# The last batch element in two halves of its tokens, and sums of 8 by TensorE in three groups of sixteen

## The chip, the cores and the metric

One core of a Trainium2 chip runs the whole kernel. The metric is the device time of one execution in microseconds. The kernel before took 3622.65 us, the median of three runs (3621.72 to 3628.54).

## What is computed

The input x has 8 batch elements of 512 tokens with 256 features. Each element goes through four steps, each with a layer norm in front and added back to x:

```
x = x + attention_a(layernorm(x))   # per token: 16 heads; q, k, v have 64 numbers each
x = x + ffn(layernorm(x))
x = x + attention_b(layernorm(x))   # over the tokens: 16 heads of 16, causal
x = x + ffn(layernorm(x))

# attention_a, for each token and head, with 64 queries and 64 keys that are single numbers:
scores[q, k] = Q[q] * K[k] / 8, masked to k <= q
attn[q] = sum_k softmax(scores)[q, k] * V[k]

# ffn (1024 hidden, ternary weights):
h = silu(w1 x * s1) * (w2 x * s2);  h = gelu(h1 h * s);  h = gelu(h2 h * s);  w3 h * s3
```

Attention A mixes nothing between tokens: it takes the features of one token alone. Attention B needs all earlier tokens of its element. The first FFN needs its own tokens alone.

## The kernel before

**Two programs in one order.** Attention A runs in groups: a group is one element b, one tile i of 128 tokens and one set g of four heads, so an element has 16 groups (`self.todo` in `AttentionA.__init__`, L722). Everything that follows attention A (first FFN, attention B, second FFN, written as Python generators `ffn` and `attention_b`) belongs to the element before, and is called the B stream here. The order of instructions on PE, DVE, ACT and POOL is written out by hand.

**Slots.** A table (`G['order']`, with one of its own for the first element) gives each step of a group a slot. Group n starts at slot 12 n; `slot(t)` calls the steps that are due, of several groups at once, in the table's order. A group's steps run from about slot -8 (`project`, the q, k and v products) to slot 36 (`new_x`, which writes the group's part into x). After each slot the main loop at the end of `fast_path` advances the B stream: each `yield` gives a number of units, `step_of` scales them by `pace`, and the loop goes on until the units spent reach `total` (304.8 for an element's 192 slots) times the slots gone, 33 slots and one element late.

**Attention A in a group.** The triangle of 64 x 64 scores is cut into squares of 32, 16, 8, 4, 2 and 1 (`units`). `scores` multiplies queries with keys (on POOL for the large squares, on DVE for the unit of 8 and below, whose tile is `ws`), `exps` is ACT's exponential, `weigh` multiplies with values on DVE. Then the sums over keys. For squares of 32 and 16 a DMA that adds (`halve`) first folds a tile in two; then `fold` on POOL, `gather` (L1047, a reduction on DVE), or `sums32` (L918): 16 transposing products against the identity that add up in PSUM, a copy by ACT (`keep_sums`), a transpose back (`turn_sums`) and one addition on DVE (`add32`). The squares of 8 and 4 are summed by `gather` on DVE and added to the accumulator `acc` by POOL (`adds`, L1063). `invert` and `divide` end the softmax; `turn_group`, `keep_att`, `project_out` and `new_x` turn the result, apply Wo and write x. The PSUM tile `bank` has two halves, taken and freed by these steps in turn. The weights of a set of heads are loaded on SP when its last tile has been projected (`load_w`, `load_wo`), so four times in an element.

**The B stream.** `ffn` makes for each pair of hidden tiles the gate products (L1293), two layers of 1024 x 1024 (L1365; h is held as a high and a low part, so both layers together are 256 products of 512 columns) and the third (L1398). Weights come in pieces of 1 MB by POOL's DMA queue (L1162), with three buffers; each piece serves 32 products. Hidden tiles and normed inputs are blocks of a pool with seven buffers (`hp`). `Normed` makes the layer norm tile by tile, in steps that `flush` releases. In the second FFN of the last element the weights are also compared with their first copy in full precision (`fits`).

Of the kernel before, what the change touches and what calls it, by code (L numbers as in the profile page):

```python
# [46 lines left out]
 'order': [[8, 'scores', 2, 1, 2], [10, 'exps', 2], [22, 'small_squares'], [20, 'add16'], [-120, 'load'],  # L47
           [-26, 'normalise'], [6, 'exps', 1], [13, 'sums32', 0], [23, 'adds', 3], [32, 'turn_group'],
           [22, 'keep_sums', 2], [16, 'keep16'], [9, 'weigh', 1], [-1, 'scores', 0, 0, 2], [11, 'fold', 0],
           [12, 'turn16'], [6, 'halve', 0], [11, 'scores', 3, 0, 1], [-30, 'ahead'], [14, 'sums16'],  # L50
           [22, 'add32', 2], [12, 'weigh', 2], [21, 'turn_sums', 2], [34, 'project_out'],
           [4, 'scores', 1, 1, 2], [-8, 'project'], [10, 'halve', 1], [36, 'new_x'], [25, 'divide'],
           [13, 'weigh', 3], [7, 'scores', 2, 0, 2], [15, 'turn_sums', 0], [17, 'fold', 2], [32, 'keep_att'],
           [-5, 'keep_qk'], [12, 'halve', 2], [13, 'keep_sums', 0], [18, 'add32', 0], [18, 'gather', 3],
           [-22, 'turn_x'], [24, 'invert'], [13, 'gather', 1], [16, 'adds', 1], [20, 'sums32', 2],
           [12, 'exps', 3], [4, 'weigh', 0], [3, 'exps', 0], [1, 'scores', 1, 0, 2], [-22, 'keep_x'],
           [0, 'scores', 0, 1, 2]],
# [3 lines left out]
           'order': [[21, 'small_squares'], [23, 'adds', 3], [21, 'sums32', 2], [-23, 'turn_x'],  # L61
                     [29, 'divide'], [0, 'scores', 0, 1, 2], [4, 'scores', 1, 0, 2], [15, 'turn16'],
                     [26, 'invert'], [19, 'add32', 0], [6, 'scores', 2, 0, 2], [6, 'halve', 0],
                     [-1, 'scores', 0, 0, 2], [-27, 'normalise'], [9, 'fold', 0], [7, 'exps', 1],
                     [10, 'exps', 2], [20, 'gather', 3], [15, 'turn_sums', 0], [4, 'weigh', 0],
                     [23, 'turn_sums', 2], [15, 'weigh', 3], [-120, 'load'], [-30, 'ahead'], [16, 'keep16'],
                     [10, 'scores', 3, 0, 1], [-21, 'keep_x'], [17, 'adds', 1], [19, 'sums16'],
                     [23, 'add32', 2], [8, 'weigh', 1], [10, 'halve', 1], [36, 'new_x'],
                     [4, 'scores', 1, 1, 2], [13, 'weigh', 2], [-5, 'keep_qk'], [6, 'scores', 2, 1, 2],
                     [14, 'exps', 3], [31, 'turn_group'], [21, 'add16'], [21, 'keep_sums', 2],  # L70
                     [15, 'gather', 1], [32, 'keep_att'], [13, 'fold', 2], [14, 'sums32', 0],
                     [14, 'keep_sums', 0], [-8, 'project'], [34, 'project_out'], [13, 'halve', 2],
                     [2, 'exps', 0]],
# [3 lines left out]
 'pace': {'gate': 1.8, 'attn': 0.65, 'wait': 1.354, 'w3': 1.05, 'out': 0.95, 'turn': 0.997},  # L77
 'total': 304.842,
# [9 lines left out]
       'proj': 21}}  # L88
# [244 lines left out]
def fast_path(ctx: ExitStack, tc: tile.TileContext, k, t, flag):  # L333
# [305 lines left out]

    def kind(b, n_u):  # L640
        c = G["first"] if b == 0 and "first" in G else G
        return c["sum"][n_u // 2] if n_u in (0, 2) else c.get("sum16", "dve")

    def reds(b):
        return (G["first"] if b == 0 and "first" in G else G).get("red", [])

    def on(b):
        return (G["first"] if b == 0 and "first" in G else G).get("on", [])

    def p16(b):  # L650
        return (G["first"] if b == 0 and "first" in G else G)["p16"]
# [4 lines left out]
    def pieces(w, n, off, nsq, cols, b, n_u, parts):  # L656
# [7 lines left out]
        if n < 16:  # L664
# [42 lines left out]

    class AttentionA:
# [3 lines left out]
        def __init__(self):  # L712
# [9 lines left out]
            self.todo = [(b, i, g) for b in range(NB) for g in range(NG) for i in range(NT)]  # L722
# [3 lines left out]
        def load_w(self, b, g):  # L726

            if b < NB:
                wqv = wp.tile([P, DC, 2 * GW], F32, tag="wqv", name=f"wqv_{b}_{g}")
                nc.sync.dma_start(wqv.rearrange("p c f -> p (c f)"), wqv_d[g])  # L730
                wk = wp.tile([P, DC, GW], F32, tag="wk", name=f"wk_{b}_{g}")
                nc.sync.dma_start(wk.rearrange("p c f -> p (c f)"), wk_d[g])
                self.w[b, g] = wqv, wk

        def load_wo(self, b, g):
            if b < NB:
                wo = wp.tile([P, GW // P, D], F32, tag="wo", name=f"wo_{b}_{g}")
                nc.sync.dma_start(wo, t.wo[g * GW : (g + 1) * GW].rearrange("(c p) f -> p c f", p=P))
                self.wo[b, g] = wo

        def slot(self, t):

            now = []
            for lo, hi, order in TABLES:
                for place, (slot, what, args) in enumerate(order):
                    late = 8 if what in ("normalise", "turn_x", "keep_x") and t - slot in (12, 20) else 0
                    n, r = divmod(t - slot - late, 12)
                    if r == 0 and lo <= n < hi and (late == 0 or t - slot == 20):
                        now.append((place / len(order), what, self.todo[n] + args))
            for _, what, args in sorted(now, key=lambda p: p[0]):  # L750
# [44 lines left out]
        def project(self, b, i, g):  # L795
# [20 lines left out]
            if i == NT - 1:  # L816
                self.load_w(b + (g + 1) // NG, (g + 1) % NG)
# [111 lines left out]
        def sums16(self, b, i, g):  # L929
# [4 lines left out]
            self.take(1, 0, 1)  # L934
# [824 lines left out]
```

## Time and profile before

| | |
|---|---|
| median of three runs | 3622.65 us |
| profiled execution | 3620.43 us, its span 3618.6 us |
| busy: DVE, PE, POOL, ACT | 86%, 84%, 82%, 69% of the span |
| granted TensorE clock, mean | 0.916 |
| DMA | 665 MB, 184 GB/s |
| last `new_x` of attention A ends | 3347.5 us |
| first gate product of the last element's first FFN | 3365.6 us |
| its end, the start of the second FFN, the end of the span | 3451, 3518, 3618.6 us |

Each row of the groups names a source line, an engine and an operation, its tiles (out<-in), shapes and count; then busy time, the mean of one, and the idle time of that engine just before it with what ended it. PE's busy time is modelled: a product's listed length holds its way through the array, so how fast products follow each other is read from their starts or from a chain row's length over its count. In the chain of waits each row is a start, a length and what ran.

### The profile page before, as it was taken

The numbers are of one execution on the slowest core, as the hardware profiler recorded it, in microseconds if no ns is written. First come the engines' busy times: TensorE is split into PE (matmuls) and PEld (weight loads), VectorE is DVE, ScalarE is ACT, GpSimd is POOL, SyncE is SP. The second block draws the span as 40 slices with busy tenths as digits, with TensorE's granted clock in tenths as the row PEclk, the third lists the DMA queues.
The fourth block names the chain that finished last, engine by engine and source line by source line (L and its number), as shares of the span: only waits on it lengthen the run. The fifth ranks groups of instructions, "written<-read, shape, count | busy, mean of one in ns | idle before, by whom it ended". The sixth has DMA issues, their size and how long they took to land.

```text
span 3618.6 us, 42449 instructions
## 1 busy us (share of the span) xinstructions
PE 3048.9 (84%) x14468; PEld 2168.6 (60%) x14468; DVE 3124.0 (86%) x3844; ACT 2505.2 (69%) x3488; POOL 2971.8 (82%) x2682
## 2 busy tenths in 40 slices
PE   7765698798887998888987988879888889878998
PEld 4544475476645766466754766457664667556756
DVE  7999998999889998999988998899989998896227
ACT  4544686687767787687866877668866878665453
POOL 7999988888898989989898888989889888885000
PEclk8878799898998999998998989989999999989999
DMA  9978897688877988689876888769877788767414
GB/s 240 200 160 165 178 228 163 149 215 194 206 165 167 231 206 185 141 204 213 224 167 144 217 191 204 167 155 232 195 190 150 193 208 209 175 146 221 131 53 170
DMA packets 117038, 665.34 MB, mean 184 GB/s; under 512 B 12742, under 2 KB 30665, under 8 KB 43467
## 3 DMA queue, kind: packets, MB, share of 16 engines
q0 software_dynamic: 80640, 587.24, 71.1%
q1 hardware_dynamic: 35896, 75.02, 6.0%
q8 instruction: 116, 1.90, 0.2%
q14 instruction: 110, 0.90, 0.1%
q10 hardware_dynamic: 276, 0.27, 0.0%
HBM read 251.18 MB, written 8.65 MB: 72 GB/s over the span
## 4 chain that ended last, share of the span: by engine, by line
PE 33%; DVE 22%; POOL 17%; ACT 14%; issue 9%; DMA 5%; ACTq 0%; POOLq 0%; SPq 0%; DVEq 0%
POOL w L855 8%; PE ph L1365 8%; DVE w L890 6%; DVE red L1047 5%; DMA w<-w 5%; PE pw L1293 4%; POOL acc L1063 3%; PE pyb L1523 3%; ACT w L878 3%; DVE ws L855 3%; PE pqkb L1444 3%; PE bank L918 3%; PE psb L1511 2%; POOL w L897 2%; PE qv L808 2%
## 5 line engine op out<-in xcount | busy, mean ns | idle before, releaser
L855 POOL TENSOR_TENSOR w<-k 128x1024 f32<-128x1024 f32 x768 | 1617.6, 2194 | 44.2 <-DVE red L1047 23.0
L1365 PE MATMUL ph<-h,hidden 128*128 128x512 f32 x4096 | 1019.6, 403 | 6.5 <-DVE h L1277 2.4
L890 DVE TENSOR_TENSOR w<-w,qv 128x1024 f32<-128x1024 f32 (+1 forms) x624 | 890.2, 1458 | 83.9 <-ACT w L878 83.8
L1365 PEld LDWEIGHTS ph<-h,hidden 128*128 128x128 f32 x4096 | 766.4, 190 | 186.7 <-issue 21.0
L878 ACT ACTIVATE w<-w 128x2048 f32<-128x2048 f32 x384 | 734.6, 1915 | 138.5 <-POOL w L855 136.5
L897 POOL DMA_DIRECT2D w<-w x384 | 352.3, 918 | 193.3 <-DVE w L890 94.7
L1293 PE MATMUL pw<-xnt,gate 128*128 128x512 f32 (+2 forms) x1152 | 346.4, 452 | 153.4 <-ACT silu L1268 99.3
L1047 DVE TENSOR_REDUCE red<-w 128x256 f32<-128x2048 f32 x240 | 426.8, 1778 | 23.7 <-DMA w<-w 22.0
L1047 DVE TENSOR_REDUCE red<-ws 128x256 f32<-128x2048 f32 (+1 forms) x256 | 435.6, 1742 | 0.0
L1063 POOL TENSOR_TENSOR acc<-acc,red 128x256 f32<-128x256 f32 x496 | 392.1, 791 | 29.5 <-DVE red L1047 11.0
L1293 PEld LDWEIGHTS pw<-xnt,gate 128*128 128x128 f32 x1152 | 236.3, 225 | 242.1 <-ACT silu L1268 124.0
L918 PE MATMUL bank<-ident,w 128*128 128x128 f32 x2304 | 322.6, 301 | 52.1 <-ACT x L1114 26.4
L855 DVE TENSOR_TENSOR ws<-qv,k 128x1024 f32<-128x1024 f32 (+3 forms) x512 | 300.0, 647 | 76.9 <-POOL acc L1063 76.8
L918 PEld LDWEIGHTS bank<-ident,w 128*128 128x128 f32 x2304 | 298.3, 158 | 80.0 <-ACT x L1114 39.2
L890 DVE TENSOR_TENSOR ws<-ws,qv 128x1024 f32<-128x1024 f32 (+3 forms) x512 | 294.9, 636 | 32.0 <-ACT ws L878 32.0
L905 POOL TENSOR_TENSOR w<-w 128x1024 f32<-128x1024 f32 x112 | 280.2, 2502 | 50.7 <-DMA w<-w 50.6
L808 PE MATMUL qv<-wqv,xnta 128*128 128x512 f32 x512 | 269.9, 653 | 27.3 <-DVE ws L890 22.0
L878 ACT ACTIVATE ws<-ws 128x1920 f32<-128x1920 f32 x128 | 233.1, 1821 | 76.2 <-DVE ws L855 72.6
L1331 DVE TENSOR_TENSOR h<-ph,h 128x512 fp32r<-128x512 f32 x256 | 167.8, 681 | 90.3 <-ACT ph L1327 84.1
L1518 ACT ACTIVATE eb<-psb 128x512 f32<-128x512 f32 (+3 forms) x503 | 181.9, 459 | 89.2 <-PE psb L1515 88.9
L1326 ACT ACTIVATE h<-ph,s_sb 128x512 fp32r<-128x512 f32 x256 | 176.6, 690 | 94.2 <-PE ph L1365 92.2
L1069 DVE RECIPROCAL acc<-acc 128x256 f32<-128x256 f32 x128 | 223.1, 1743 | 3.9 <-POOL acc L1063 3.9
(163 smaller groups left out, 4867.5 us busy)
## 6 DMA issues: line engine op xcount, KB each, us to landing
w<-w POOLq DMA_DIRECT2D x384, 1024.0 KB, 7.6
hidden<-in_h POOLq DMA_DIRECT2D x128, 1024.0 KB, 6.4
gate<-in_w12p POOLq DMA_DIRECT2D x32, 1024.0 KB, 6.7
w<-in_w3p POOLq DMA_DIRECT2D x16, 1024.0 KB, 6.0
wqv<-wqv_d SPq DMA_DIRECT2D x31, 512.0 KB, 3.9
wo<-in_wo SPq DMA_DIRECT2D x32, 256.0 KB, 7.4
w<-in_h SPq DMA_DIRECT2D x8, 1024.0 KB, 6.9
wk<-wk_d SPq DMA_DIRECT2D x31, 256.0 KB, 6.2
```

Of the source, the lines that this page charges most:

```text
L808: nc.tensor.matmul(qv.rearrange("p j f -> p (j f)"), xnt[:, c, :], wqv[:, c, :], start=(c == 0), stop=(c == DC - 1),)
L855: eng.tensor_tensor(e, rows(q).to_broadcast(shape), columns(kt[:, 0]).to_broadcast(shape), ALU.mult)
L878: nc.scalar.activation(e, e, AF.Exp, scale=C**-0.5)
L890: nc.vector.tensor_tensor(ev, e, columns(qv[:, 1]).to_broadcast(list(e.shape)), ALU.mult)
L897: nc.gpsimd.dma_start(w[:, :2048], w[:, 2048:], accum_op=ALU.add)
L905: nc.gpsimd.tensor_tensor(w[:, :1024], w[:, :1024], w[:, 1024:2048], ALU.add)
L918: nc.tensor.matmul(bank_half(G["half"][4])[:, :P], w[:, j * P : (j + 1) * P], ident, start=(j == 0), stop=(j == n - 1), is_transpose=True,)
L1047: nc.vector.tensor_reduce(red, self.columns_of(w, n, off, nsq), AX.X, ALU.add)
L1063: (nc.vector if what == "psum" or what in on(b) else nc.gpsimd).tensor_tensor(rows, rows, part.rearrange("p a (x i) -> p a x i", i=n), ALU ...
L1069: nc.vector.reciprocal(acc[:, 0, :], acc[:, 0, :])
L1293: nc.tensor.matmul(pj[:, toks], w[:, m % 4, j, c, :], xs[:, p, c, toks], start=(p == 0 and c == 0), stop=(p == 1 and c == DC - 1),)
L1365: nc.tensor.matmul(pss[j], w[:, j, c, :], h_in(p, c), start=(p == 0 and c == 0), stop=(p == 1 and c == MC - 1),)
```

## The change

**Sums of 8.** In three places of an element's sixteen groups (4, 13 and 14, from the second element on) the squares of 8 are laid out column by column and summed by TensorE: 16 transposing products into half 1 of `bank` (`sums8`, slot 18), a copy by ACT (`keep8`, 19), two transposes back (`turn8`, 20) and an addition on DVE (`add8`, 23). `gather` skips them there, and POOL's addition goes with it.

**The last element.** Its groups run in another order: tiles 0 and 1 for all four sets of heads, then tiles 2 and 3. Weights are loaded whenever the set of heads changes, so eight times. Its first FFN runs twice, on 256 tokens each (names with `_high` for the second), with its weights loaded twice; the low half stands behind the second FFN of the element before, in the B stream. The stream's rate is 1.2 times as high from the slot where element 6 is due (`last`). Attention B has parameters for halves too, but is called for all tokens.

**Orders.** Both tables are rewritten, mostly in the sequence of entries of one slot. Entries that do work and change slot: in the main table `scores 1,1` 4 to 1, `divide` 25 to 27, `keep_att` 32 to 33; in the first element's `scores 2,1` 6 to 8, `exps 2` 10 to 11, `weigh 3` 15 to 14, `turn_sums 2` 23 to 22, `project` -8 to -7, the layer norm's `normalise` -27 to -26 and `turn_x` -23 to -22. `pace['wait']` goes from 1.354 to 1.422, `total` from 304.842 to 305.821.

```diff
+ 'kinds': {'3': {}, '4': {'sum8': 'pe'}, '13': {'sum8': 'pe'}, '14': {'sum8': 'pe'}, '0': {}},
+ 'last': 1.2}
...
+    def kinds(b):
+        if b == 0 and "first" in G:
+            return G["first"]
+        return {**G, **G.get("kinds", {}).get(str(place[0]), {})}
...
+        if n == 8 and kind8(b) == "pe":
+            e, ev = (
+                w[:, a * SMALL + off : a * SMALL + off + nsq * n * n].rearrange("p (j x i) -> p j x i", j=n, i=n)
+                for a in range(2)
+            )
+            yield e, ev, lambda v: of_rows(v).unsqueeze(1), lambda v: of_cols(v).rearrange("p x j -> p j x").unsqueeze(3)
...
+    HALVES = range(NT // 2), range(NT // 2, NT)
...
-            self.todo = [(b, i, g) for b in range(NB) for g in range(NG) for i in range(NT)]
+            self.todo = [(b, i, g) for b in range(NB - 1) for g in range(NG) for i in range(NT)]
+            self.todo += [(NB - 1, i, g) for some in HALVES for g in range(NG) for i in some]
...
-            if i == NT - 1:
-                self.load_w(b + (g + 1) // NG, (g + 1) % NG)
+            self.new_weights(b, i, g, self.load_w)
...
+        def sums8(self, b, i, g):
+            if kind8(b) == "dve": return
...
+            self.take(h, 0, 1)
+            for r in range(2):
+                for j in range(8):
+                    nc.tensor.matmul(
+                        bank_half(h)[:, r * P : (r + 1) * P], w[:, r * SMALL + j * P : r * SMALL + (j + 1) * P], ident,
+                        start=(j == 0 and r == 0), stop=(j == 7), is_transpose=True, skip_group_check=True,
+                    )
...
+        def keep8(self, b, i, g):
...
+            nc.scalar.copy(self.live["sums8"], bank_half(h))
+            self.free(h, 0, 1)
+        def turn8(self, b, i, g):
...
+            for r in range(2):
+                nc.tensor.transpose(bank_half(h)[:, r * P : (r + 1) * P], s8[:, r * P : (r + 1) * P], ident)
+        def add8(self, b, i, g):
...
+            rows = acc.rearrange("p a (x t) -> p a x t", t=16)[..., 8:]
+            nc.vector.tensor_tensor(
+                rows, rows, bank_half(h).rearrange("p (a x i) -> p a x i", a=2, i=8), ALU.add
+            )
...
+                if n == 8 and kind8(b) == "pe": continue
...
-                    yield from ffn()
+                    for _ in range(1 + (b == NB - 1)):
+                        yield from ffn()
...
-    def ffn(u, b, xt, nx, after):
+    def ffn(u, b, xt, nx, after, some=range(NT)):
+        nt = len(some)
+        share, all_toks = nt / NT, slice(some[0] * P, (some[-1] + 1) * P)
...
                         nc.tensor.matmul(
-                            pss[j],
+                            pss[j][:, all_toks],
                             w[:, j, c, :],
-                            h_in(p, c),
+                            h_in(p, c)[:, all_toks],
...
-                        yield step_of("h", 0.225 * len(step))
+                        yield step_of("h", 0.225 * share * len(step))
...
+        b = NB - 1
+        xt = a.x[b]
+        for some in HALVES:
+            more = "_high" * (some[0] > 0)
+            while (b, some[-1]) not in a.ready:
+                yield 1
+            if some[0] > 0:
+                for i in some:
+                    head(b, i)
+            u = f"1_{b}" + more
+            yield from ffn(u, b, xt, nx[u], lambda i: tile(f"b{b}", b, "b", i), some)
+        u = f"b{b}"
+        yield from attention_b(b, xt, nx[u], lambda i: tile(f"2_{b}", b, "f", i))
+        u = f"2_{b}"
+        yield from ffn(u, b, xt, nx[u], lambda i: None)
...
-            while spent * 12 * NT * NG < total * (at + 1 - 12 * NT * NG - 33):
+            due = at + 1 - 12 * NT * NG - 33
+            due += (G.get("last", 1.5) - 1) * max(0, due - 12 * NT * NG * (NB - 2))
+            while spent * 12 * NT * NG < total * due:
                 spent += next(done)
```

## The prediction

> **What bounds the kernel now.** I read the page first: busy shares, and the slices for where they change.
>
> ```profile
> PE 3048.9 (84%) x14468; PEld 2168.6 (60%) x14468; DVE 3124.0 (86%) x3844; ACT 2505.2 (69%) x3488; POOL 2971.8 (82%) x2682
> ...
> DVE  7999998999889998999988998899989998896227
> ...
> POOL 7999988888898989989898888989889888885000
> ```
>
> DVE and POOL sit at eight to nine tenths until slice 37, then POOL stops: two programs. To 3305 us attention A and the FFN/attention B stream share the core; after it only PE's stream is left. The busy time by stage (columns: PE, PEld, DVE, ACT, POOL, granted clock, DMA share, GB/s) shows both:
>
> ```profile
> 2449.10:2848.80 399.70, 338.41 (x1642) 240.91 (x1641) 360.27 (x450) 299.05 (x414) 355.58 (x320) 0.93 0.80 188
> 2873.00:3276.70 403.70, 342.75 (x1640) 242.80 (x1640) 358.83 (x441) 297.86 (x411) 353.97 (x319) 0.92 0.78 183
> ...
> 3365.60:3451.00 85.40, 84.66 (x368) 69.27 (x368) 23.89 (x42) 34.30 (x56) 4.97 (x10) 0.98 0.35 114
> 3451.00:3518.00 67.00, 62.53 (x449) 33.10 (x450) 9.20 (x42) 39.92 (x103) 7.87 (x19) 0.96 0.10 32
> 3518.00:3618.60 100.60, 87.71 (x390) 71.99 (x389) 72.40 (x68) 35.07 (x57) 4.22 (x8) 0.94 0.51 174
> ```
>
> Fifteen groups of a middle or the last element take 400 us with DVE 90% and POOL 89% busy; PE's 85% is modelled length. The last three rows are the last element's first FFN (85 us, PE 99% busy), attention B and second FFN, with attention A gone. Then the chain of waits through the hand-over (start, length):
>
> ```profile
> 3302.98 12.13 DMA w<-w
> 3325.58 16.35 PE ph L1365 x72
> 3365.59 16.40 PE pw L1293 x64
> 3381.99 58.03 PE ph L1365 x256
> 3440.02 7.27 PE pot L1398 x32
> ```
>
> From 3318 on it is PE alone. 58.03/256 = 227 ns per 512-column product, one after the other. Last, the groups by shape:
>
> ```profile
> L1047 DVE TENSOR_REDUCE red<-ws 128x256 f32<-128x2048 f32 x128 | 291.4, 2277 | 0.0
> L1063 POOL TENSOR_TENSOR acc<-acc,red 128x256 f32<-128x256 f32 x384 | 340.8, 888 | 18.2 <-DVE red L1047 8.1
> L918 PE MATMUL bank<-ident,w 128*128 128x128 f32 x2304 | 322.6, 301 | 52.1 <-ACT x L1114 26.4 <-DMA w<-w 17.1 <-ACT ws L878 4.4
> L1162 POOL DMA_DIRECT2D hidden<-in_h x128 | 101.4, 792 | 112.8 <-PE ph L1365 67.6 <-PE pw L1293 43.4 <-PE pof L1419 1.5
> ```
>
> The first is the sum of 8 on DVE (2.28 us), the second the POOL addition it needs (0.89 us).
>
> **The change, part by part.**
>
> **1. The tail: the first FFN in two halves.** I count from the last sums32 (16 transposes at 3305.2 us, slot 1537) to the end of the last element's first FFN, 3451: 146 us. In PE's new order all of element 6's second FFN stands ahead of that point, 196 products of 227 ns (44 us) earlier than before; behind it come the low half, then the high half.
>
> A product of 256 columns is not in the trace. The same line starts one each 227 ns at 512 columns, 174 at 384 and 111 at 128, so between 114 (half) and 174; on the line from 384 to 512, 121 ns. [...]
>
> High half: gate 64 x 121 = 7.7, say 10, as ACT and DVE per hidden tile (0.84 and 0.89 us, the 512-column 690+579 and 748+673 ns less 213 or 267 ns each) nearly fill PE's 0.97; two layers of 128 x 121 = 15.5; third product 3.9; output 3; normalisation 1.5. Two layer ends: the cover for the last GELU pair is 24 x 121 = 2.9 us, not 5.4, and the tile xnt_b7, made at the end of the low half, now holds one of seven h blocks while the high half needs all seven, so the third block of each layer waits for the last pair of products. No row shows this: between 0 and the whole chain, 4 x 0.47 + 2 x 0.42 = 2.7 us; I take 3 with the shorter cover, 6 for both. Sum 10 + 31 + 3.9 + 3 + 1.5 + 6 = 55.
>
> Low half, from the same point: normalisation 2; gate 15, since DVE's last reduction stands among its gate instructions and waits for the halving DMA (12.13 us above), as it does today; layers 31 + 6; attention A's last transposes and projections 2; third product and output 6. Sum 62.
>
> So 62 + 55 = 117 in place of 146: **-29 us**. The rest of the tail (67 + 100 us) has the same instructions. DMA: a 1 MB weight now serves 32 x 121 = 3.9 us, 270 GB/s; alone one lands in 5.1 us and is issued 1.5 periods, 5.8 us, ahead. It just fits; if not, some 0.5 us per weight, 5 us.
>
> **2. What is crowded into the last element.** Ahead of slot 1537 come those 44 us of PE products, 16 GELU subtractions on DVE (16 x 0.69 = 11 us), 32 GELUs (22 us) and table loads on ACT, five or six weight issues on POOL (x 0.79 = 4). The stream runs at 1.2 times its rate from slot 1377. PE has room: 192 us of B products per element (two FFNs of 82, attention B 28) plus 67 of A, at the trace's start-to-start times, are 62% of 420 us and become about 72%. DVE is where it shows: 11 us less the sums of 8 (5.6) are +5; POOL likewise +2; DMA share is 0.91 in the FFN layers and gets more weights, to which I give 5 us. Bounds: 0 (all in idle time), 44 (PE on the path throughout). I take **+10 us**, near the DVE figure.
>
> Moves with it: wqv, wk and wo are fetched for eight stretches of two groups, not four of four: 12 more SP issues, 4 MB. A fetch has a 26 us group for the 6 to 7 us the page gives it: nothing; without that cover 6 us x 4. SP holds nothing urgent behind them. On POOL the last divide stands behind the issue of the fourth hidden block, which waits for the low half's first layer pair; its consumer on PE stands 108 products (13 us) later: nothing.
>
> **3. Sums of 8 on TensorE, 21 groups (three places, elements 1 to 7).** Removed per group: 2.28 us DVE, 0.89 POOL. Added: 16 transposes, a copy (ACT, 0.38 as L1089's shape), two transposes, one DVE addition out of PSUM (128x256; the 128x128 one takes 0.28, SBUF ones 0.41; I take 0.41). DVE nets -1.87 us. On PE the start-to-start median of L918 is 109 ns, so 18 x 109 = 2.0 us. Here a rule speaks against: the Trainium skill, "TensorE: Matmul & The Clock Gate", Part 4, says that transposes do not count as PE activity for the clock gate, so runs of them would stay at half clock. The row mostly disagrees, but its ninetieth percentile is 213 ns, and the granted clock in the gate stages is 0.83. By the rule, 18 x 213 = 3.8 us per group. I take the row.
>
> If DVE alone were the bound, elements 1 to 6 would gain 18 x 1.87 = 34 us; if PE's queue passes its 2.0 us on, they lose 2. The new wait: sums8 needs the PSUM half that DVE's add32 frees in the same slot, and FFN products and the next projection queue behind it on PE. DVE idles some 37 us per element waiting for ACT, POOL and DMA, so only part passes: I take 0.8 us per group, **-14 us**.
>
> **4. Orders, pace, total.** Per engine the working entries keep their sequence, but divide goes behind one score product and adds 1 behind a halving on POOL; in the first element some move by a slot or two. The stream rate changes by 0.3%. Estimate 0, between -8 and +8.
>
> Sum: -29 + 10 - 14 + 0 = **-33 us** on the profiled execution of 3620.4 us (span 3618.6), 3587. The median shown is 2.2 us above it: **3590 us**.
>
> **The rivals.**
>
> A. The DVE saving passes whole and the last element absorbs its load: -29 + 0 - 34 = -63, 3560. For it: DVE at 90%. Against: waits for POOL and ACT alternate with DVE's work. Chance 0.14.
>
> B. The crowding costs what it brings: the last element stretches by the full 44 us, sums of 8 gain 14: -29 + 44 - 14 = +1, 3624. For it: PE's in-order queue, DMA near full in the FFN layers. Against: 62% real load. Chance 0.09.
>
> C. Slower: sums8 becomes the bound of its groups. The transposes run at half clock and hold PE's queue: 3.8 - 1.87 = +1.9 us in each of 21 groups, +40; with +10 and -29, +21, 3644. It decides once a group loses over 0.9 us net (19/21). For it: clock 0.83 at two of the places, PE waits of up to 4.3 us in gate stages. Against: DVE and POOL both lose work there. Chance 0.13.
>
> D. The low half only changes places: attention A ends later by what the tail loses. The fixed order speaks against it: 250 of its 352 products stand ahead of A's last projection. It is inside B's time and chance.
>
> **How the numbers follow.** My own case 0.64, A 0.14, B 0.09, C 0.13. A measurement of this kernel tells about 0.2%, 7 us, from no change: faster is below 3615, slower above 3630. Of my case 0.61 lies below 3615 and 0.03 within; B is split, 0.04 within, 0.03 faster, 0.02 slower; C is 0.12 slower and 0.01 within. Faster 0.78, same 0.08, slower 0.14. My case alone spans 3572 to 3612. The range takes in most of A and B and stops where C begins, 3556 to 3630: about 0.05 lies below, 0.14 above.
>
> **What would show it.** Right: L1047's 128x2048 form over ws down from 128 to 107; the second chain row of 512-column ph products replaced by 256-column ones starting each 121 ns; the high half's first pw to last pof near 54 us where the whole took 85; middle elements 2 to 4 us shorter. Wrong: elements 1 to 6 longer, with PE waiting in sums8 (C); the last element's fifteen groups at 430 us or more (B); 256-column products at 150 ns or more, or the high half waiting for its weights.

## The result, and the profile after

The changed kernel takes 3649.6 us (median of four runs, 3641.6 to 3650.8) against 3623.3 for the kernel before, measured beside it: a ratio of 1.0063 (95% interval 1.0047 to 1.0079), 26 us slower. The prediction was 3590 us, faster. The profiled execution took 3649.5 us, its span 3647.5.

The first lines of the page again, busy time and the slices of DVE and POOL:

```profile
PE 3079.6 (84%) x15198; PEld 2223.9 (61%) x15198; DVE 3093.4 (85%) x3876; ACT 2533.5 (69%) x3570; POOL 2959.9 (81%) x2672
...
DVE  7999997999889988889889998889988888788326
...
POOL 7999988889898989989888888889888887777200
```

DVE lost 30.6 us of busy time, and the span grew by 28.9. So the work that the change removes did go, and waiting took its place. POOL's last full slices have sevens where it had eights and nines.

Busy time by stage (columns: PE, PEld, DVE, ACT, POOL, granted clock, DMA share, GB/s): fifteen groups of element 6 and of element 7, the high half of the first FFN, attention B, the second FFN:

```profile
2459.90:2867.30 407.40, 345.39 (x1684) 248.23 (x1683) 356.82 (x450) 299.84 (x416) 352.53 (x317) 0.92 0.79 184
2891.40:3329.40 438.00, 389.26 (x1858) 281.43 (x1857) 363.80 (x452) 321.97 (x442) 355.18 (x320) 0.93 0.78 189
3426.00:3478.00 52.00, 49.04 (x368) 46.42 (x368) 16.74 (x50) 25.75 (x62) 7.74 (x17) 0.93 0.62 208
3478.00:3545.00 67.00, 62.09 (x443) 32.67 (x442) 8.78 (x40) 37.98 (x98) 6.88 (x16) 0.95 0.10 32
3545.00:3647.50 102.50, 87.39 (x391) 71.44 (x391) 72.80 (x69) 35.43 (x59) 4.51 (x9) 0.95 0.49 170
```

The second row is 438 us long where the kernel before had 403.7: the last element's groups got 34 us longer with almost the same work on DVE (363.8 for 358.8) and POOL (355.2 for 354.0). The third row, now the high half alone, has shrunk as forecast (52 us where the whole took 85, forecast near 54); the last two are within 2 us of what they were.

The chain of waits through the hand-over (start, length):

```profile
3359.41 12.81 DMA w<-w
3387.59 16.79 PE ph L1447 x140
...
3410.21 9.59 PE ph L1447 x80
3419.80 3.37 PE pot L1480 x28
3431.09 9.95 PE pw_high L1375 x64
3441.04 30.95 PE ph_high L1447 x256
3472.62 3.03 PE pot_high L1480 x23
```

In place of one row of 58 us for 256 products of 512 columns there are the low half's rows, and one of 30.95 us for the high half: 121 ns per product. Everything in this chain starts late: the folding DMA of the last group begins at 3359 us where it began at 3303.

The groups by shape (the first row is of before, the others of after):

```profile
L855 POOL TENSOR_TENSOR w<-k 128x1024 f32<-128x1024 f32 x768 | 1617.6, 2194 | 44.2 <-DVE red L1047 23.0 <-PE bank L918 18.2 <-ACT k L825 1.5
L883 POOL TENSOR_TENSOR w<-k 128x1024 f32<-128x1024 f32 x768 | 1582.8, 2179 | 82.8 <-PE bank L946 49.2 <-DVE red L1125 30.2 <-DVE ws L918 2.2
L1141 POOL TENSOR_TENSOR acc<-acc,red 128x256 f32<-128x256 f32 x363 | 292.4, 805 | 24.7 <-DVE red L1125 8.5
L1125 DVE TENSOR_REDUCE red<-ws 128x256 f32<-128x2048 f32 x107 | 243.8, 2278 | 0.0
```

The reductions over `ws` are down from 128 to 107 and the additions from 384 to 363. The first two rows are new to the reading: POOL's score products wait 49.2 us for PE (`bank` at L946, the `sums32` products, which read the previous tile) where they waited 18.2 us before.

One account for all kernels below. A group's start is taken as the time at which DVE first writes its accumulator `acc` (the products of the squares of 1): how late the last element starts (column 1), how long its first fifteen groups take (2), what is left from the start of the sixteenth to the end of the span (3). Medians are of all runs; a profiled execution can lie some microseconds from them (the runs of the kernel before scatter from 3607.6 to 3637.1), so totals are read from medians and columns for where the time sits. Column 1 alone scatters by some 10 us: e4 and e6 do not differ until after that point, and have 2872.9 and 2882.9.

| kernel | median us | ratio to before, 95% | 1 | 2 | 3 |
|---|---|---|---|---|---|
| before | 3623 to 3625 | | 2873.0 | 403.7 | 341.9 |
| after | 3649.6 | 1.0047 to 1.0079 | 2891.5 | 438.1 | 318.0 |
| e1_no_sums8 | 3651.1 | 1.0043 to 1.0086 | 2904.2 | 435.6 | 316.3 |
| e2_whole_last | 3643.5 | 1.0035 to 1.0070 | 2895.2 | 409.9 | 341.7 |
| e3_only_sums8 | 3636.0 | 1.0017 to 1.0039 | 2889.6 | 404.0 | 343.4 |
| e4_only_halves | 3633.6 | 1.0015 to 1.0038 | 2872.9 | 437.8 | 315.0 |
| e5_sums8_late | 3623.1 | 0.9988 to 1.0005 | 2877.4 | 400.7 | 341.4 |
| e6_halves_rate1 | 3640.0 | 1.0024 to 1.0057 | 2882.9 | 401.4 | 354.5 |
| e7_tile_order | 3624.1 | 0.9990 to 1.0021 | 2876.6 | 401.0 | 344.1 |
| e8_only_orders | 3647.4 | 1.0056 to 1.0108 | 2886.9 | 407.9 | 344.0 |
| e9_orders_oldpace | 3631.1 | 1.0014 to 1.0043 | 2880.2 | 404.6 | 343.6 |
| e10_orders_att32 | 3632.1 | 1.0005 to 1.0041 | 2885.3 | 401.5 | 346.4 |
| e11_orders_pool | 3653.1 | 1.0055 to 1.0105 | 2912.8 | 407.9 | 341.9 |
| e12_sums8_gate | 3619.2 | 0.9980 to 1.0003 | 2868.4 | 404.0 | 341.1 |
| e13_old_orders | 3658.7 | 1.0072 to 1.0123 | 2889.2 | 448.3 | 314.5 |
| e14_mended | 3635.3 | 1.0021 to 1.0040 | 2875.1 | 436.4 | 317.4 |
| e15_add8_late_alone | 3634.2 | 1.0018 to 1.0042 | 2879.8 | 404.1 | 340.4 |
| e16_sums8_gate_again | 3618.9 | 0.9977 to 0.9995 | 2867.4 | 403.3 | 342.2 |

So after against before: the last element starts 18.5 us later, its groups take 34.4 longer, the rest is 23.9 shorter. Sum +29.0, the difference of the spans.

### The profile page after: what moved, and what is told of

The parts are those of the page before. It is cut to its first block, busy times and chain, and to the rows that moved or that the text cites. A ratio compares the mean times of both kernels' runs of the same rounds, so it can differ in the third digit from the quotient of the medians.

```text
span 3647.5 us, 44023 instructions
## 1 busy us (share of the span) xinstructions
PE 3079.6 (84%) x15198; PEld 2223.9 (61%) x15198; DVE 3093.4 (85%) x3876; ACT 2533.5 (69%) x3570; POOL 2959.9 (81%) x2672
## 5 line engine op out<-in xcount | busy, mean ns | idle before, releaser
L883 POOL TENSOR_TENSOR w<-k 128x1024 f32<-128x1024 f32 x768 | 1582.8, 2179 | 82.8 <-PE bank L946 49.2
L1447 PE MATMUL ph<-h,hidden 128*128 128x512 f32 (+1 forms) x4096 | 989.8, 396 | 0.8 <-DVE h L1359 0.8
L1447 PEld LDWEIGHTS ph<-h,hidden 128*128 128x128 f32 x4096 | 746.2, 189 | 167.9 <-issue 21.0
L1375 PE MATMUL pw<-xnt,gate 128*128 128x512 f32 (+3 forms) x1152 | 341.7, 448 | 152.3 <-ACT silu L1350 93.7
L1141 POOL TENSOR_TENSOR acc<-acc,red 128x256 f32<-128x256 f32 (+1 forms) x475 | 376.1, 792 | 24.8 <-DVE red L1125 8.5
L1125 DVE TENSOR_REDUCE red<-ws 128x256 f32<-128x2048 f32 (+1 forms) x235 | 389.7, 1696 | 0.0
L946 PE MATMUL bank<-ident,w 128*128 128x128 f32 x2304 | 319.3, 299 | 39.4 <-ACT x L1191 21.4
L946 PEld LDWEIGHTS bank<-ident,w 128*128 128x128 f32 x2304 | 295.7, 157 | 66.0 <-ACT x L1191 33.3
L1413 DVE TENSOR_TENSOR h<-ph,h 128x512 fp32r<-128x512 f32 (+1 forms) x256 | 163.8, 666 | 91.2 <-ACT ph L1409 91.2
L1408 ACT ACTIVATE h<-ph,s_sb 128x512 fp32r<-128x512 f32 (+1 forms) x256 | 173.2, 677 | 69.3 <-PE ph L1447 67.6
```

The source lines that it names most:

```text
L883: eng.tensor_tensor(e, rows(q).to_broadcast(shape), columns(kt[:, 0]).to_broadcast(shape), ALU.mult)
L946: nc.tensor.matmul(bank_half(G["half"][4])[:, :P], w[:, j * P : (j + 1) * P], ident, start=(j == 0), stop=(j == n - 1), is_transpose=True,)
L1125: nc.vector.tensor_reduce(red, self.columns_of(w, n, off, nsq), AX.X, ALU.add)
L1141: (nc.vector if what == "psum" or what in on(b) else nc.gpsimd).tensor_tensor(rows, rows, part.rearrange("p a (x i) -> p a x i", i=n), ALU ...
L1375: nc.tensor.matmul(pj[:, toks], w[:, m % 4, j, c, :], xs[:, p, c, toks], start=(p == 0 and c == 0), stop=(p == 1 and c == DC - 1),)
L1447: nc.tensor.matmul(pss[j][:, all_toks], w[:, j, c, :], h_in(p, c)[:, all_toks], start=(p == 0 and c == 0), stop=(p == 1 and c == MC - 1),)
```

## Experiments

### The parts one by one: e1 to e4

The first four take the change apart: without the sums of 8, without the halves, the sums of 8 alone, the halves alone.

```diff
 e1, in the changed kernel:
- 'kinds': {'3': {}, '4': {'sum8': 'pe'}, '13': {'sum8': 'pe'}, '14': {'sum8': 'pe'}, '0': {}},
+ 'kinds': {},
```

> The changed kernel with the sums of 8 back on DVE in all places; halves, orders and rates stay. Theory S (the sums of 8 lengthen the middle elements: they took 18 us more from the first group to the last element's first, and the last element shares in it): about 3625, with the last element's first group back at 2873 us. Theory O (the new orders and pace did it, the sums of 8 gave what DVE lost): 3650 to 3660, the last element's first group at 2891 or later. Under both the last element's fifteen groups stay over 425 us if the crowding is what stretches them (404 before).

```diff
 e2, in the changed kernel (one first FFN for the last element, its groups in the old sequence):
- self.todo = [... for b in range(NB - 1) ...]; self.todo += [... for some in HALVES ...]
+ self.todo = [(b, i, g) for b in range(NB) for g in range(NG) for i in range(NT)]
- 'last': 1.2}
+ 'last': 1.0}
```

> The changed kernel with the last element as before: tiles in their old order, one first FFN of 512 tokens in the tail, no faster rate; sums of 8 and new orders stay. If the crowding of the last element costs more than the halves save there (34 us longer against a tail 24 us shorter), this gains some 10 us: 3640. If the halves are worth what was forecast (29 less 10), it loses 19: 3668.

```diff
 e3, the kernel before with the code of sums8, in its own table:
+ [18, 'sums8'], [19, 'keep8'], [20, 'turn8'], [23, 'add8'],
+ 'kinds': {'4': {'sum8': 'pe'}, '13': {'sum8': 'pe'}, '14': {'sum8': 'pe'}}
```

> The kernel before with the sums of 8 alone (same three places and slots, put into the old tables). Theory S: 3640 to 3645, as the middle elements lengthen by 3 us each. Theory O: 3605 to 3615, the DVE saving of 1.87 us in 21 groups partly passes.

```diff
 e4, the changed kernel with both tables, pace and total of before:
- 'kinds': {... 'sum8' at places 4, 13, 14 ...}
+ 'kinds': {}
```

> The kernel before with the halves alone (old tables, old pace, sums of 8 on DVE, rate 1.2 in the last element). Forecast of the prediction: -29 + 10 + 6 = 3608 to 3612. If the crowding stretches the last element as the profile of the changed kernel shows (34 us against 24 us saved): 3630 to 3635.

Measured: 3651.1, 3643.5, 3636.0 and 3633.6 us, before 3623.7. No part alone is a gain; the halves cost 10 us and the sums of 8 cost 12. In the changed kernel, though, removing the sums of 8 does not help (3651.1 for 3649.6), and removing the halves gives back some 6 us of 26. What e2 still holds is the orders and the sums of 8, at +20 us. The prediction had costed the orders at 0. e3 fell between its two expected times: neither theory had the size.

### The halves: e6 and e7

```diff
 e6, in e4:
- 'last': 1.2}
+ 'last': 1.0}
```

> The kernel before with the halves alone, and the B stream's rate in the last element at 1.0 in place of 1.2. Theory R (a unit of B stream moved into the last element's attention A lengthens it by the same time, so the rate does not matter): the last element's fifteen groups back near 405 us (438 at 1.2), the tail 25 to 35 us longer, the total 3628 to 3640 as with 1.2. Theory T (the stretch comes from the other tile order and its loads): fifteen groups stay above 420 us and the total is 3645 or more.

```diff
 e7, the kernel before with the last element's groups in the new sequence and its weights loaded eight times; one whole first FFN, rate 1.0:
- self.todo = [(b, i, g) for b in range(NB) for g in range(NG) for i in range(NT)]
+ self.todo = [(b, i, g) for b in range(NB - 1) for g in range(NG) for i in range(NT)]
+ self.todo += [(NB - 1, i, g) for some in HALVES for g in range(NG) for i in some]
```

> The kernel before with one thing changed: attention A of the last element runs tiles 0 and 1 for all heads, then 2 and 3, with eight loads of its weights; the first FFN stays whole and in the tail, rate 1.0, sums of 8 on DVE, old tables. Theory R: 3622 to 3626, the order costs nothing. Theory T: the last element's groups take 20 us or more longer than the 404 of before, 3640.

Measured: 3640.0 and 3624.1 us, before 3624.6. The busy time by stage, the last element's fifteen groups and what follows them, of e4 (rate 1.2):

```profile
2872.90:3310.70 437.80, 385.94 (x1817) 278.00 (x1816) 367.00 (x452) 322.56 (x442) 357.45 (x322) 0.92 0.78 190
3310.70:3625.80 315.10, 280.34 (x1748) 224.79 (x1746) 155.42 (x245) 155.24 (x315) 62.88 (x93) 0.96 0.56 179
```

of e6 (rate 1.0):

```profile
2882.90:3284.40 401.50, 341.47 (x1640) 241.81 (x1639) 358.45 (x441) 297.95 (x411) 354.37 (x319) 0.92 0.81 193
3284.40:3638.90 354.50, 320.80 (x1924) 256.29 (x1923) 163.47 (x257) 167.54 (x337) 64.79 (x97) 0.97 0.55 174
```

and of e7, the fifteen groups alone:

```profile
2876.60:3277.60 401.00, 341.51 (x1639) 242.31 (x1638) 358.50 (x440) 297.76 (x411) 354.07 (x319) 0.92 0.81 194
```

Between e6 and e4 the higher rate moves 177 products into the fifteen groups, 44.5 us of PE's busy time there (40.5 less in the tail). It shortens the tail by 39.4 us and lengthens the fifteen groups by 36.3. Inside the groups PE's share of busy time is only 85% in e6, and DVE's 89%; yet nine tenths of what is moved in is paid there. DVE gets 8.6 us of work, POOL 3.1, ACT 24.6 (74% busy in both): the 36 us are not DVE's or POOL's work. My reading is that the engines run in order and wait for each other by turns, so that a program with three of them 85% to 90% busy had no room for a second one to run faster. The two runs show the price; by which waits it is paid, and what ACT's part is, they do not separate.

e7 clears the rest: the order of the tiles and four more fetches of each weight cost nothing (401.0 us for 403.7).

The halving itself has a price too. At equal rate the part after the fifteen groups is 354.5 us in e6 against 341.9 before. Its chain of waits:

```profile
3381.89 30.72 PE ph L1448 x256
3412.61 3.37 PE pot L1481 x28
...
3423.97 9.64 PE pw_high L1376 x64
3433.61 30.95 PE ph_high L1448 x256
```

The two layers take 30.72 + 30.95 = 61.7 us, where the whole ones took 58.0, and between the low half's last third product and the high half's first gate product lie 8.0 us: output, addition to x, and the high half's normalisation, with nothing of the last element to put beside them. 3.6 + 8.0 make 11.6 of the 12.6 us.

### The orders: e8 to e11

```diff
 e8, the kernel before with the new tables, pace and total, and nothing else:
- 'order': [[8, 'scores', 2, 1, 2], ... [25, 'divide'], ... [32, 'keep_att'], ...]
+ 'order': [[-26, 'normalise'], ... [27, 'divide'], ... [33, 'keep_att'], ...]
- 'pace': {... 'wait': 1.354 ...}, 'total': 304.842
+ 'pace': {... 'wait': 1.422 ...}, 'total': 305.821
```

> The kernel before with the new tables, pace and total alone. From the run without sums of 8 (3651) less the one with the halves alone (3634): 3641, and the last element's first group at 2900 us. If the orders only hurt together with the halves: 3624.

```diff
 e9, in e8:
- 'wait': 1.422 ... 'total': 305.821
+ 'wait': 1.354 ... 'total': 304.842
```

> The new tables alone (as the run with only the orders, 3647), but with the old pace and total. If the tables do the harm: 3643 to 3650. If the B stream's new pace does: 3624.

```diff
 e10, in e8, main table:
- [33, 'keep_att']
+ [32, 'keep_att']
```

> The new tables, pace and total alone, with keep_att of the main table back from slot 33 to 32, so that two slots lie again between ACT's copy and PE's project_out at 34. PE's wait for that copy grew from 9 to 24 us in elements 1 to 6 of the run without sums of 8. If that wait is the harm: 3628 to 3635; if not: 3643 to 3650.

```diff
 e11, in e8, main table, POOL's entries where they were:
- [27, 'divide'] ... [1, 'scores', 1, 1, 2] ... [22, 'add32', 2] behind [10, 'halve', 1]
+ [25, 'divide'] ... [4, 'scores', 1, 1, 2] ... [22, 'add32', 2] ahead of [10, 'halve', 1]
```

> The new tables, pace and total alone, with POOL's entries of the main table in their old slots and sequence (divide at 25 ahead of the score products, scores 1,1 at slot 4, the addition of unit 2 ahead of the second halving); keep_att stays at 33. If POOL's sequence is the harm: 3624 to 3632; if not: 3643 to 3650.

Measured: 3647.4, 3631.1, 3632.1 and 3653.1 us; before 3624.6 beside e8, 3624.2 beside the others. The new tables and the new pace alone cost 23 us, nearly as much as the changed kernel lost. POOL's sequence shows no part in it. Two other edits do: either `keep_att` back at 32 or the old pace takes off 15 to 16 us, and leaves 7 to 8. So neither is the cause by itself; it takes both to make 23.

The place is seen in what PE waited for ahead of `project_out` (the row of the group and that of the line, then idle time in us and times; this idle time adds up PE's and that of its weight loads, which run side by side, and the group's row has PE's alone). Of the kernel before:

```profile
L1101 PE MATMUL bank<-wo,att 128*128 128x256 f32 x512 | 155.4, 431 | 13.6 <-ACT att L1089 9.1 <-ACT sums L980 4.5
L1101 PE MATMUL bank<-wo,att x512: 377/379/797, 71.4 to 3346.3; 128*128 128x256 f32 x171
...
  ACT att L1089: 23.1, 31
```

of the changed kernel:

```profile
L1179 PE MATMUL bank<-wo,att 128*128 128x256 f32 x512 | 152.8, 425 | 27.6 <-ACT att L1167 23.1 <-ACT sums L1008 4.5
L1179 PE MATMUL bank<-wo,att x512: 377/379/797, 70.5 to 3409.4; 128*128 128x256 f32 x171
...
  ACT att L1167: 51.4, 39
```

of e8, and of e10:

```profile
  ACT att L1166: 61.9, 47
```

```profile
  ACT att L1166: 16.4, 23
```

PE's own wait there is 9.1 us before, 23.1 after, 27.7 in e8 and 6.1 in e10. `keep_att` is ACT's copy of the turned result into `att`, and `project_out`, at slot 34, multiplies `att` with Wo. From 32 the copy has two slots to get through ACT's queue, from 33 one, some 2.2 us at 420 us per 192 slots. Behind `project_out` PE's queue holds the next `sums32`, and POOL's score products wait for that: 18.2 us before, 49.2 after, 39.7 in e8, 23.6 in e10. So one slot on an engine that is 69% busy (ACT) holds up one that is 84% busy (PE), and POOL, 82% busy, waits longer for PE.

These waits are no measure of the loss. In e9 the row for `att` has 56.7 us (PE alone 24.5), about as in e8, and POOL waits 43.3 for PE, yet the kernel loses only 7 us, between the two times expected; in e16 below, the fastest kernel, POOL waits as long for PE:

```profile
L883 POOL TENSOR_TENSOR w<-k 128x1024 f32<-128x1024 f32 x768 | 1622.9, 2200 | 58.0 <-PE bank L946 45.4 <-DVE red L1125 11.2 <-ACT k L853 1.2
```

The other half of the loss comes with the pace. What e9 undoes is two numbers: `total` lets the stream run 0.3% faster, and `wait` makes each step of waiting for a layer norm count 5% more units. So the B stream falls on other slots in every element. Why that costs 16 us beside `keep_att` at 33, no wait in these profiles singles out; it stays open.

### The sums of 8: e5, e15, e12, e16

```diff
 e5, in e3:
- [20, 'turn8'] ... [23, 'add8']
+ [22, 'turn8'] ... [24, 'add8'], [24, 'invert']
```

> The kernel before with the sums of 8 alone, as in the run with only the sums of 8, but DVE's addition add8 stands right ahead of invert (slot 24, not 23) and the transposes back at slot 22, not 20. Theory W (DVE's saving is lost in add8's own wait: it idled 35 us ahead of 21 add8, mostly for POOL's additions into the same accumulator and for PE, and PE idled 27 us for the copy): most of both waits go, and the time is 3610 to 3618. Theory Q (the 18 products in PE's queue cost it, wherever add8 stands): 3633 to 3639, as before.

```diff
 e15, in e3: turn8 stays at 20
- [23, 'add8']
+ [24, 'add8'], [24, 'invert']
```

> The kernel before with the sums of 8 at places 4, 13 and 14, add8 late (slot 24) but turn8 still at slot 20, where PE idled 27 us for ACT's copy. If DVE's wait ahead of add8 was the loss: 3621 to 3626. If PE's wait was: 3632 to 3638.

```diff
 e12 and e16 (one kernel, measured twice), in e5:
- 'kinds': {'4': {'sum8': 'pe'}, '13': {'sum8': 'pe'}, '14': {'sum8': 'pe'}}
+ 'kinds': {p: {'sum8': 'pe'} for p in ('2', '3', '12', '13')}
```

> The kernel before with the late form of the sums of 8 at places 2, 3, 12 and 13, which fall into the B stream's gate stages, where PE waits for DVE and ACT, in place of 4, 13 and 14. If DVE's saving is only worth something where DVE sets the pace: 28 groups x 1.87 us = 52 us at most, half of it is 3600; if the saving turns into another wait there too: 3618 to 3626.

> The same kernel as the late sums of 8 at places 2, 3, 12 and 13, in more rounds, because its interval just reached no change: 3617 to 3621 if the gain of 5 us is one, 3623 to 3625 if not.

Measured: e5 3623.1, e15 3634.2, e12 3619.2 and e16 3618.9 us. What e3 waited for ahead of `turn8` (on PE) and ahead of `add8` (on DVE), then one of the 21 groups in order of time (start, length, in brackets the engine's idle time before it):

```profile
L1090 PE MATMUL bank<-ident,sums x42: 272/300/330, 487.5 to 3317.8; 128*128 128x128 f32 x42
...
  ACT att L1167: 27.1, 42
```

```profile
L1097 DVE TENSOR_TENSOR acc<-acc,bank x21: 420/421/426, 493.8 to 3323.1; 128x256 f32<-128x256 f32 x21
...
  POOL acc L1141: 17.4, 12
  PE bank L537: 14.6, 8
  ACT xn L617: 3.4, 1
```

```profile
484.95 0.37 ACT L1081 COPY sums<-bank 128x256 f32<-128x256 f32 x1 [0.19 <-PE bank L1070]
487.03 0.37 ACT L1167 COPY att<-bank 128x256 f32<-128x256 f32 x1 [1.15 <-PE bank L1163]
487.45 0.44 PE L1090 MATMUL bank<-ident,sums 128*128 128x128 f32 x2 [0.46 <-ACT att L1167]
```

`turn8` does not wait for its own input: `keep8` (L1081) has ended 1.7 to 5.1 us before it in all 21 groups. It starts 0.05 us after ACT's copy `keep_att` (L1167) of the group before. Slots 20 and 32 of two groups in sequence are one slot, and in it `turn_group` on PE, `keep_att` on ACT and `turn8` on PE stand one behind the other, so PE stands still while ACT copies: 11.1 us in all, 0.46 us in most groups (the 27.1 adds 16.0 us of the weight loads' idle time beside it). The two use different halves of `bank`; why the program waits there was not looked into. DVE waits another 35 us, half of it for POOL's additions into the same `acc`, most of the rest for PE's last product of `project_out` (L537). e15 takes DVE's wait away and leaves PE's. Its row of `turn8`, and who waited for its `add8`:

```profile
  ACT att L1167: 27.1, 42
```

```profile
L1097 DVE TENSOR_TENSOR acc<-acc,bank x21: 410/413/415, 495.3 to 3316.4; 128x256 f32<-128x256 f32 x21
...
  POOL w L925: 65.4, 21
```

DVE's 35 us are gone and the median does not move (3634.2 for 3636.0). e5 differs from e15 in `turn8`'s slot alone. It removes PE's wait as well, and 11 us go: PE's wait was the loss, or at least what came of `turn8`'s place. Its 3623.1 us lie between the two times expected: the stall went, and no gain came.

In the changed kernel itself neither wait is there, since `keep_att` at 33 now stands behind `turn8`: PE waits for nothing at `turn8`, DVE 2.7 us at `add8`. (In exchange `keep_att` waits for `turn8`, 18.7 us in 13 groups.) So its sums of 8 are not delayed, and they still bring little. e5 shows why: it has no stall at either place, 21 x 1.7 us less DVE work, and the time of the kernel before (ratio 0.9988 to 1.0005). DVE's wait at the subtraction behind the second GELU (total us, times, longest) before, in e5, in e1 and in the changed kernel, and what waits for `add8` in e5:

```profile
DVE h L1331 <- ACT ph L1327: 84.1, 68, 7.1
DVE h L1413 <- ACT ph L1409: 135.9, 88, 7.1
DVE h L1413 <- ACT ph L1409: 51.7, 64, 3.4
DVE h L1413 <- ACT ph L1409: 91.2, 82, 5.4
```

```profile
  POOL w L925: 64.6, 21
```

That GELU, on ACT, follows PE's stream. The wait is 52 us longer in e5 than before, and 40 us longer in the changed kernel than in e1, which is the same without the sums of 8; the work saved on DVE is 36 us in both. I read it so: DVE comes earlier to the subtraction behind a GELU, and the stream's rate, not DVE, sets when that instruction can run. POOL's folding DMA waits 3.1 us in each of the 21 groups for DVE's queue. At places 2, 3, 12 and 13, chosen because the stream is in its gate stage there, with 28 groups in place of 21, DVE's wait behind the GELUs is smaller (103.7 us in e16), and the kernel is 5 us faster than before: 3618.9 us, ratio 0.9986 (0.9977 to 0.9995). That is the one version that beats both kernels. Places and number were changed together, so which of the two does it stays open. One thing more differs: the granted clock. It is 0.920 to 0.929 in all 22 runs of e16, and 0.909 to 0.919 in the 57 of before. Over the stream's gate stages it is 0.88 where it was 0.83, the mean of fourteen, with only the sums' products added on PE; one such stage before and in e16 (columns as above):

```profile
1954.00:1994.30 40.30, 28.44 (x119) 20.97 (x117) 35.35 (x48) 30.86 (x36) 33.54 (x30) 0.83 0.73 182
1951.40:1992.30 40.90, 31.21 (x153) 24.03 (x151) 32.99 (x49) 31.18 (x38) 32.48 (x29) 0.87 0.73 180
```

These stages are no shorter for it, so whether the clock has a part in the 5 us is open too.

### Together: e13 and e14

```diff
 e13, the changed kernel with both old tables, old pace and total, sums8 entered as in e3

 e14, the changed kernel, main table, pace and total:
- [33, 'keep_att'] ... [20, 'turn8'] ... [23, 'add8'] ... 'wait': 1.422 ... 'total': 305.821
+ [32, 'keep_att'] ... [22, 'turn8'] ... [24, 'add8'], [24, 'invert'] ... 'wait': 1.354 ... 'total': 304.842
```

> The changed kernel with the old tables, pace and total (sums of 8 in the early form and halves stay). If the parts simply add (12 for the sums of 8, 10 for the halves): 3646. If the sums of 8 and the halves share a loss, as they do beside the new orders: 3634 to 3640.

> The changed kernel with three things undone: keep_att of the main table at slot 32, old pace and total, and the late form of the sums of 8 (turn8 22, add8 24 ahead of invert). If the causes found are the whole of it, only the price of the halves is left: 3631 to 3636. If something else stays: 3643 or more.

Measured: 3658.7 and 3635.3 us, before 3624.0. e14 undoes the two causes found in the orders and takes the late places for the sums of 8: 14 us come back, and what is left, 11 us, is what the halves cost alone (e4, 10 us). So these three edits and the halves account for the loss, in size. e13 is the miss: 12 us for e3 and 10 for e4 should have made some 22 and made 35; its last fifteen groups take 448.3 us, where the halves alone have 437.8, and its `turn8` has the wait of e3 again. Why the two cost more together was not shown. So the parts do not add, and beside halves and sums of 8 the new orders even gain: the changed kernel, with them, is 8 to 9 us faster than e13 (four runs each).

## Why the prediction was wrong

The parts do not add, so what one costs depends on the sequence in which they are built up. Three sequences, each run against the kernel before that was measured beside it:

| first | second | third |
|---|---|---|
| orders and pace +23 (e8) | sums of 8 -3 (e2) | halves +6 (after) |
| halves +10 (e4) | orders and pace +17 (e1) | sums of 8 -1 (after) |
| sums of 8 +12 (e3) | halves +22 (e13) | orders and pace -8 (after) |

The -3, +6 and -1 are inside the intervals. Three of the four terms failed, and no single one gave the wrong sign: with the crowding as measured in place of +10 the forecast sum is about 0, and sums of 8 that gain nothing and orders that cost something make the rest.

1. **The tail was right.** From the last `sums32` to attention B's first product it is 149.4 us before and 115.6 after, -34 for -29, where the prediction's own sum for the new stretch was 117. Some of this closeness is luck: the low half took 65 us for 62, the high half 51 for 55. The product of 256 columns takes 121 ns as read off the line from 384 to 512; the high half's gate 9.95 us for 10; its layers 30.95 for 31 + 6. The 6 us of stalls at the layer ends did not come: the weight loads of `ph_high` waited 0.2 us for ACT. In their place came 7.9 us between the low half's last third product and the high half's gate, for which the terms for output and normalisation gave about 4.

2. **The crowding was the mis-sized term: +10 forecast, about +42 measured.** Cut at the last `sums32`, where the prediction cut it, the last element takes 474.6 us up to there, where it took 432.2 (42 us more, 34 of them in the fifteen groups; with the halves alone, in e4, it is 37 us more). The bounds, 0 and 44, held, and the price is all but the upper one. The choice within them failed: the forecast took what was added to DVE's queue, +5, and 5 for the DMA as the price, since PE had a real load of 62%. e6 and e4 show the price with nothing else changed: 36 us in, 39 out. The prediction's own mark for rival B, 430 us or more for the fifteen groups, was passed (438), and B's size is what e6 and e4 show. B's time of 3624 still assumed -14 for the sums of 8.

3. **The sums of 8: forecast -14, worth nothing that is clear of the noise.** DVE's busy time in elements 1 to 6 fell from 2295.0 to 2264.2 us, 1.7 us in each of 18 groups for 1.87 forecast, so the work was counted right. The factor that turned it into time, 0.8 us per group, failed: DVE's saving became a longer wait behind the GELUs (e5, and e1 against after). Rival A, that it passes whole, is further off still. The weighed rule was that of the Trainium skill, "TensorE: Matmul & The Clock Gate", Part 4, that transposes do not count as activity for the clock gate. Here the transposing products of `sums8` start 109 ns apart, 110 at the ninetieth percentile, so taking the row was right. e16, whose gate stages get such products and no others and have a clock of 0.88 for 0.83, speaks against the rule as well; no run here has transposes alone. Rival C's sign was right (the middle elements are 3.5 us longer each), its mechanism wrong: the transposes were not held by a half clock, and the middle elements are as late without the sums of 8 (e1).

4. **The orders and the pace: forecast 0, between -8 and +8.** They cost 23 us alone and 17 beside the halves, and gain 8 beside halves and sums of 8. The prediction noted each entry's sequence on its own engine, which had hardly changed, and asked what each new place stood behind. It did not ask how far the consumer on the other engine stands: `keep_att` at 33, `project_out` at 34. The trace of before had the row: PE already waited 9.1 us there for ACT, with two slots of room. A wait that is already seen at two slots cannot be costed at nothing for one. The pace, costed at nothing for its 0.3%, is the other half, and its mechanism stays open.

No rival held the orders as a cause. That the middle elements would be 2 to 4 us shorter was the mark that failed first: over elements 1 to 6 they are 20.9 us longer in all.

## What to carry to other kernels

In this kernel, where several in-order engines pass work to each other, busy shares of 85% to 90% left no room: in such a place cost work that is moved in at its whole length on the stream, until a run at another rate shows less. In an order written by hand, list for every moved entry the slots to its producer and to its consumer on the other engines, and read the wait that the trace already shows at that place; a table that "only" shifts entries by one slot deserves the same working as the change it comes with. And take a saving on one engine into the sum only after naming what that engine waits for next. When reading a wait, look at which copy ended just before it, not at the one that the data would suggest: `turn8` waited for `keep_att`. A wait that grew is not yet a loss: e9 has the longer waits of PE and POOL and e16 that of POOL, with little of the time or none.

## What the runs showed of the hardware

- A TensorE product of 256 columns in this stream starts every 121 ns, with a weight load of its own for each (listed at 192 ns, overlapped). The weights, 1 MB for each 3.9 us, kept up: no product of the high half waited for them, at 208 GB/s over it.
- Sixteen transposing products that add up in one PSUM tile start 109 ns apart, among other products. Adding 18 or 34 transposing products to a gate stage went with a granted clock of 0.88 there in place of 0.83 (e16).
- The folding DMA of the last group took 12.8 us in the hand-over, as before the change (12.1).
- Runs of the same kernel scatter by up to 0.5% either way, so an effect of 5 us took 22 runs beside 57 of before (e16) to separate from nothing; 12 beside 22 (e12) had left it open, at 0.9980 to 1.0003.
